# Two f32 parts in place of three bf16 parts, and two more counted groups in each layer, in a two-layer graph network on one core

## The chip, the core and the metric

The kernel runs on one of the eight cores of one Trainium2 chip. The metric is device time in microseconds (us). The core has TensorE (PE; its weight loads are listed apart as PEld), VectorE (DVE), ScalarE (ACT), GpSimd (POOL) and SyncE (SP), which issues DMAs.

## What is computed

Two mean-aggregating graph layers (SAGE), a linear layer, a residual and a layer norm. There are 12,500 nodes with 256 features and 200,000 edges, sorted by target; targets are drawn as 12500 u^2, so that low nodes have many edges.

```python
def sage(x, src, dst, W_l, b_l, W_r):
    agg = segment_sum(x[src], dst, 12500)
    deg = segment_sum(ones, dst, 12500)
    return (agg / maximum(deg, 1))[:, None] @ W_l + b_l + x @ W_r     # mean of the neighbours
h = relu(sage(x, src, dst, W1_l, b1, W1_r))
h = relu(sage(h, src, dst, W2_l, b2, W2_r))
out = layernorm(x + h @ W3 + b3)
```

## The kernel before

The edges form 1563 tiles of 128, the nodes 98 blocks of 128. In each layer the sums over neighbours come in one of two ways.

**Counted groups.** The first nodes, in groups of 256 (DN), are done by products. For a group, `count` builds a matrix of how often each of the 12,544 source rows points to each of its 256 nodes: per edge tile some VectorE comparisons (`pick`, `low`, `aft`; L738 to L746), matmuls into `count_ps` (L765 to L780) and one ScalarE copy into `counts` (L782). `product` then multiplies all 98 blocks of rows with it. The rows are f32, and the counts are whole numbers below 256. So that the sum is exact, `exact` splits each row into three bf16 parts, stored in DRAM (`x3_d`, `h3_d`); a block and a group take 3 parts x 2 halves of the features = 6 matmuls of 256 columns (L707). Layer 1 has five such groups (HG1), layer 2 eight (HG).

In layer 2 a pass does two groups at once: group 4 + i from `counts` in SBUF, and group i, whose counts layer 1 stored in DRAM (`stored`, L831) and which are streamed back into `spare` (L697). Both groups' matmuls load the same rows anew. The first pass runs alone, the two after it beside the counting of groups 6 and 7.

**Gathers.** The edges of all other nodes go in rounds of four tiles. GpSimd gathers the source rows by indirect DMA into one of four buffers `got` (L262); TensorE sums them with four strip matmuls `part_ps` (L274) and, after a ScalarE copy `some`, with the matmuls of `summed` (L290), and VectorE adds the result into a ring `sums` (L304).

**Order.** TensorE and GpSimd run in the order in which the program is written. `layer` writes it round by round: the gather's strips first, then three parts of filler, with a piece of a finished block (`pieces`: transposes, the four weight products L925 and L930, and in layer 2 those with W3, L997) at the start of each. The filler is a list of stages; `mixed` interleaves the parts of a stage in proportion to costs written by hand (COST_DENSE, COST_DEGREES, COST_SPLIT, `count_cost`), and the rounds are shared out over the stages by those costs. In layer 1, stage 0 counts group 0 beside the splitting of the rows; stage g counts group g beside the products and degrees (L797) of group g - 1 and the storing of its counts. Eight rounds in layer 1 and fourteen in layer 2 are left for after the last stage.

**The rows' ring.** SP loads the row parts of two blocks at a time into one of four buffers (NROWS), 384 KB each (L693). A load is made to wait for the gather's strip that follows the last product from its buffer:

```python
if len(used) >= n and used[-n] < len(strips):
    tc.add_manual_dep(load.ins, strips[used[-n]], LANDED, reason="products done")
```

SP also loads and stores the blocks' rows (L896, L974, L977, L1010) and the degrees (L960, L965), in one queue.

Of the kernel before, what the change touches and what calls it, by code (L numbers as in the profile page):

```python
# [1 line left out]

# [5 lines left out]
F32 = mybir.dt.float32  # L8
F16 = mybir.dt.float16
# [14 lines left out]
P = 128  # L24
# [23 lines left out]
def by_runs(  # L48
# [55 lines left out]
    HG1, HG, DN = 5, 8, 256  # L104
# [6 lines left out]
    ROOMS = [5, 5, 7, 7] + [5] * 5 + [7] * 5 + [9] * 5 + [10] * 2  # L111
# [3 lines left out]
    def room(t):  # L115
# [15 lines left out]
    x3_d = dram.tile([P, NB, 3, D], BF16, name="x3_d")  # L131
    h3_d = dram.tile([P, NB, 3, D], BF16, name="h3_d")
    count_d = dram.tile([HG1 - 1, P, NB, DN], BF16, name="count_d")
# [7 lines left out]
    place = consts.tile([1, len(groups)], I32, name="place")  # L141
# [3 lines left out]
    key_t = [consts.tile([P, n], F32, name=f"key_t{g}") for g, n in enumerate(tiles_of)]  # L145
    after_from = [max(t, FIRST - 1) for t in lows[:HG]]
    after_t = [consts.tile([P, b - a], F32, name=f"after_t{g}")
               for g, (a, b) in enumerate(zip(after_from, highs))]
    offs = [consts.tile([1, n], I32, name=f"offs{g}") for g, n in enumerate(tiles_of)]
# [33 lines left out]
    degs = spare[0:1]  # L183
    rdeg = early.tile([P, NB], F32, name="rdeg")
# [6 lines left out]
    NROWS = 4  # L191
# [380 lines left out]
    w3_sb = weight(w3, "w3_sb", "w3")  # L572

    biases = consts.tile([P, 3, D], F32, name="biases")
    for i, b in enumerate((b1, b2, b3)):
        nc.scalar.dma_start(biases[:, i], b[None, :].to_broadcast([P, D]))
# [9 lines left out]
    split = keep.tile([P, 2, 3, D], BF16, name="split")  # L586
    counts = [keep.tile([P, NB, DN + WIDEST + WIDEST % 2], BF16, name=f"counts{i}") for i in range(2)]
    NEAR = int(at_most(FIRST)) + room(FIRST - 1)
    assert NEAR <= DN
    for c_sb in counts:  # L590
        blank = c_sb.rearrange("p s d -> p (s d)").bitcast(F32)
        nc.scalar.copy(blank, zero.to_broadcast(list(blank.shape)))
# [63 lines left out]
    def exact(t, s, rest):  # L656


        def upper(a):
            return a.bitcast(BF16).rearrange("p (n h) -> p n h", h=2)[:, :, 1]  # L660

        leaves = nc.vector.tensor_tensor(rest, t, upper(t), op=OP.subtract)
        nc.vector.tensor_tensor(s[:, 2], rest, upper(rest), op=OP.subtract)
        nc.scalar.copy(s[:, 0], upper(t))
        nc.scalar.copy(s[:, 1], upper(rest))
        return leaves

    def split_rows(b):
        t = load_rows(x, N, b, "split_sb")
        s = split[:, b % 2]  # L670
        leaves = exact(t, s, work.tile([P, D], F32, name="rest", tag="own"))
        if b < 3:
            later(leaves)
        nc.sync.dma_start(x3_d[:, b], s)

    STREAMS = 4
    streams = [spare.bitcast(BF16)[:, i * 2 * DN:(i + 1) * 2 * DN].rearrange("p (b d) -> p b d", b=2)
               for i in range(STREAMS)]
    n_streamed = 0

    def product(table3, g, c_sb, beside=None):


        nonlocal n_streamed
        ps = [dense_pool.tile([P, NC, DN], F32, name="dense_ps")]
        if beside is not None:
            ps.append(beside_pool.tile([P, NC, DN], F32, name="beside_ps"))
        for t in ps:
            nc.tensor.matmul(t, lhsT=zeros_b, rhs=c_sb[:, :NC, :DN], start=True, stop=False)
        for b in range(NB):  # L690
            if b % 2 == 0:
                rows = work.tile([P, 2, 3, D], BF16, name="rows", bufs=NROWS)
                loads = [(nc.sync.dma_start(rows, table3[:, b:b + 2]), NROWS)]  # L693
                if beside is not None:
                    stream = streams[n_streamed % STREAMS]
                    n_streamed += 1
                    loads.append((nc.sync.dma_start(stream, count_d[beside, :, b:b + 2]), STREAMS))  # L697

                for load, n in loads:
                    if len(used) >= n and used[-n] < len(strips):  # L700
                        tc.add_manual_dep(load.ins, strips[used[-n]], LANDED, reason="products done")
            counted = [c_sb[:, b, :DN]] + ([stream[:, b % 2]] if beside is not None else [])
            n = 0
            for k in range(3):
                for c in range(NC):
                    for t, d in zip(ps, counted):
                        nc.tensor.matmul(t[:, c], lhsT=rows[:, b % 2, k, c * P:(c + 1) * P], rhs=d,  # L707
                                         start=False, stop=b == NB - 1 and k == 2 and c == NC - 1)
                        n += 1
                        if n == 3 * NC and beside is not None:  # L710
                            yield COST_DENSE
            if b % 2:
                used.append(len(strips))
            yield COST_DENSE
        d_sb = work.tile([P, NC, DN], F32, name="d_sb", bufs=1)
        nc.scalar.copy(d_sb, ps[0])
        yield g, d_sb
        if beside is not None:
            b_sb = split.rearrange("p two k d -> p (two k d)").bitcast(F32)[:, :NC * DN].rearrange(
                "p (c d) -> p c d", c=NC)  # L720
            nc.scalar.copy(b_sb, ps[1])
            yield beside, b_sb

    def count(g, to):
# [7 lines left out]
        def pick(t):  # L732
# [7 lines left out]
            low = work.tile([P, LW], BF16, name="low", bufs=6)  # L740
# [3 lines left out]
            if t + 1 >= FIRST:  # L744
                aft = work.tile([P, NB], BF16, name="aft", bufs=6)
# [60 lines left out]
    COST_DENSE, COST_DEGREES, COST_SPLIT = 0.7, 1.6, 0.8  # L806
# [22 lines left out]
    def stored(g, c_sb):  # L829
        for b0 in range(0, NB, 14):  # L830
            nc.sync.dma_start(count_d[g, :, b0:b0 + 14], c_sb[:, b0:b0 + 14, :DN])  # L831
            yield 0.5

    def dense(table3, waiting, with_deg, g, c_sb, beside=None):
        made = []
        for p in product(table3, g, c_sb, beside):
            if isinstance(p, float):
                yield p
            else:
                made.append(p)  # L840
        if with_deg:
            yield from degrees(g, c_sb)
        for g, d_sb in made:
# [11 lines left out]
    assert NB % 14 == 0 and HG == 2 * (HG1 - 1)  # L855

    def stages_1(waiting):

        for g in range(HG1 + 1):
# [3 lines left out]
            else:  # L863
                parts.append((dense(x3_d, waiting, True, g - 1, counts[(g - 1) % 2]), D_1))
                if g < HG1:
                    parts.append((stored(g - 1, counts[(g - 1) % 2]), MOVED))
            yield list(parts)

    def stages_2(waiting):

        for beside, g in enumerate(range(HG1 - 1, HG)):
            parts = [(dense(h3_d, waiting, False, g, counts[g % 2], beside), D_2)]
            if HG1 <= g < HG - 1:
                parts.append((count(g + 1, counts[(g + 1) % 2]), counting(g + 1)))
            yield parts
# [78 lines left out]
    def first_block(b, agg=None):  # L954
# [21 lines left out]
        exact(h, s, own)  # L976
        nc.sync.dma_start(h3_d[:, b], s)  # L977
        yield True

    def last_block(b, agg=None):  # L980
# [8 lines left out]
        h2, _ = sage(h_t, copied, b, agg, of_ring, w2l_sb, w2r_sb, biases[:, 1], "h")  # L989
# [3 lines left out]
        nc.vector.tensor_add(x_sb, x_sb, biases[:, 2])  # L993
# [405 lines left out]
```

## Time and profile before

| | |
|---|---|
| median of 3 runs | 3284.89 us (3281.76 to 3287.56) |
| profiled execution, its span | 3281.46 us, 3279.7 us |
| mean granted TensorE clock | 0.888 |
| PE busy | 2574.5 us (79%), 18946 instructions |
| POOL busy | 1967.7 us (60%) |
| DVE busy | 1566.5 us (48%) |
| ACT busy | 1151.6 us (35%) |
| DMA | 612.56 MB, mean 187 GB/s |
| of it SP's queue, the gathers' queue | 343.33 MB, 264.37 MB |
| chain that ended last | PE 59%, issue 8%, unknown queue 7%, DVE 5%, ACT 3%, DMA 3% |

Busy time is a union over an engine's instructions. Matmuls overlap: a product of 256 columns has a mean duration of 282 ns, but the next starts earlier, so the spacing of starts is what a matmul costs. A waiting time is put down to the event that ended it. A group of instructions is given as line, engine, operation, output <- inputs, shape and number.

### The profile page before, as it was taken

How to read it: one execution, taken by the hardware profiler on the slowest of the kernel's cores; microseconds unless marked ns; L12 is line 12 of the kernel's file. 1: busy time of each engine (PE TensorE's matmuls, PEld its weight loads, DVE VectorE, ACT ScalarE, POOL GpSimd, SP SyncE). 2: the span in 40 equal slices, each digit the busy share in tenths (PEclk: the TensorE clock that was granted, in tenths of full speed). 3: DMA queues.
4: the chain of work that ended last, by engine and by line, in shares of the span. 5: the costliest groups of instructions: out<-in, count | busy, mean ns of one | idle time of the engine just before them, and what ended most of it. 6: DMA issues, size and time to landing. Idle time of an engine off the chain costs nothing.

```text
span 3279.7 us, 56146 instructions
## 1 busy us (share of the span) xinstructions
PE 2574.5 (79%) x18946; PEld 1733.1 (53%) x18946; DVE 1566.5 (48%) x5560; ACT 1151.6 (35%) x2331; POOL 1967.7 (60%) x2026
## 2 busy tenths in 40 slices
PE   4565668878878878889865887878889888888876
PEld 2122335545546656656643555556556666666654
DVE  6778675544445555555552122334345444343334
ACT  0423664444444444455441001223233333221122
POOL 6665666666665656666664666565666666556652
PEclk9766679979979989989987899989989999999998
DMA  5565668658658758647644566565556656566642
GB/s 123 164 185 171 179 205 274 209 159 262 209 156 289 225 174 266 221 144 238 222 142 122 181 183 184 176 181 166 177 167 192 184 170 183 164 200 198 204 139 84
DMA packets 375242, 612.56 MB, mean 187 GB/s; under 512 B 72111, under 2 KB 253989, under 8 KB 374949
## 3 DMA queue, kind: packets, MB, share of 16 engines
q1 hardware_dynamic: 273235, 343.33, 34.0%
q0 software_dynamic: 96768, 264.37, 26.7%
q8 instruction: 155, 2.54, 0.3%
q10 hardware_dynamic: 4946, 1.19, 0.2%
q14 instruction: 138, 1.13, 0.1%
HBM read 518.75 MB, written 89.92 MB: 186 GB/s over the span
## 4 chain that ended last, share of the span: by engine, by line
PE 59%; issue 8%; another core or an unknown queue 7%; DVE 5%; ACT 3%; DMA 3%; POOL 0%; ACTq 0%; DVEq 0%; SPq 0%; POOLq 0%
PE dense_ps L707 16%; PE part_ps L274 7%; PE count_ps L776 7%; PE beside_ps L707 6%; PE block_ps L925 6%; PE block_ps L930 5%; PE sum_ps L290 4%; PE block_ps L997 3%; PE block_ps L902 3%; DMA rows<-x_d 2%; ACT counts L782 2%; PE count_ps L780 1%; PE sum_ps L296 1%; PE dense_ps L797 1%
## 5 line engine op out<-in xcount | busy, mean ns | idle before, releaser
L262 POOL DMA_INDIRECT got<-in_x_dram,src_t x1076 | 1067.8, 992 | 649.6 <-issue 258.2
L262 POOL DMA_INDIRECT got<-h_d,src_t x940 | 897.7, 955 | 617.1 <-issue 230.8
L707 PE MATMUL dense_ps<-counts,rows 128*128 128x256 bf16 x5292 | 981.6, 282 | 58.9 <-issue 31.5
L707 PEld LDWEIGHTS <-rows 128*128 128x128 bf16 x7644 | 745.2, 101 | 327.6 <-issue 165.6
L782 ACT CAST counts<-count_ps 128x882 f32 (+3 forms) x688 | 611.3, 888 | 533.1 <-PE count_ps L776 135.6
L707 PE MATMUL beside_ps<-spare,rows 128*128 128x256 bf16 x2352 | 570.3, 282 | 24.2 <-issue 23.2
L776 PE MATMUL count_ps<-pick,low 128*128 128x490 bf16 (+2 forms) x1188 | 378.7, 371 | 145.0 <-ACT counts L782 64.3
L274 PE MATMUL part_ps<-got,one 128*32 128x257 f32 (+1 forms) x4032 | 385.4, 434 | 53.2 <-issue 21.7
L738 DVE TENSOR_SCALAR pick<-steps,key_t 128x686 bf16<-128x686 f16 (+3 forms) x816 | 332.6, 410 | 117.6 <-remote 32.1
L218 DVE TENSOR_TENSOR one<-lo_t,lane_b 128x128 f32<-128x128 bf16 x504 | 144.1, 286 | 470.7 <-remote 150.1
L284 ACT COPY some<-part_ps 128x257 f32<-128x257 f32 (+1 forms) x355 | 132.8, 374 | 643.4 <-remote 293.7
L741 DVE TENSOR_SCALAR low<-lanes,low_t 128x130 bf16<-128x130 f16 x816 | 221.0, 272 | 212.4 <-remote 72.5
L304 DVE TENSOR_TENSOR sums<-sums,sum_ps 128x256 f32 x355 | 145.6, 410 | 250.2 <-remote 110.6
L290 PE MATMUL sum_ps<-two,some 128*128 128x128 f32 x1420 | 241.1, 296 | 13.1 <-issue 8.3
L290 PEld LDWEIGHTS sum_ps<-two,some 128*128 128x128 f32 x1420 | 211.2, 207 | 32.2 <-issue 19.3
L776 PEld LDWEIGHTS <-low 128*128 128x128 bf16 x1188 | 121.1, 103 | 181.9 <-issue 62.7
L936 DVE TENSOR_TENSOR own<-block_ps,biases 128x256 f32<-128x256 f32 x196 | 82.4, 420 | 220.3 <-PE block_ps L930 106.5
L274 PEld LDWEIGHTS part_ps<-got,one 128*32 128x32 f32 x4032 | 89.1, 113 | 184.1 <-issue 161.1
L925 PE MATMUL block_ps<-w1l_sb,sums 128*128 128x256 f32 x352 | 123.5, 483 | 69.7 <-issue 31.5
L933 ACT COPY sums<-zero 128x256 f32<-128x256 f32 x170 | 68.7, 404 | 306.0 <-PE block_ps L930 142.6
L904 ACT COPY own_t<-block_ps 128x256 f32<-128x256 f32 x294 | 109.3, 375 | 183.4 <-remote 65.4
L746 DVE TENSOR_SCALAR aft<-steps,after_t 128x98 bf16<-128x98 f16 x689 | 173.6, 252 | 0.0
(184 smaller groups left out, 2678.7 us busy)
## 6 DMA issues: line engine op xcount, KB each, us to landing
rows<-x_d SPq DMA_DIRECT2D x245, 384.0 KB
rows<-h_d SPq DMA_DIRECT2D x196, 384.0 KB
count_d<-counts SPq DMA_DIRECT2D x28, 896.0 KB
spare<-count_d SPq DMA_DIRECT2D x196, 128.0 KB
x_sb<-in_x_dram SPq DMA_DIRECT2D x194, 128.0 KB
x_d<-split SPq DMA_DIRECT2D x98, 192.0 KB
h_d<-split SPq DMA_DIRECT2D x98, 192.0 KB
got<-in_x_dram,src_t POOLq DMA_INDIRECT x1076
```

Of the source, the lines that this page charges most:

```text
L262: rows = nc.gpsimd.indirect_dma_start(out=g[:, j, :D], out_offset=None, in_=self.table, in_offset=bass.IndirectOffsetOnAxis(ap=src_t[:, e: ...
L274: strip = nc.tensor.matmul(part_ps[j * W:(j + 1) * W, :width], lhsT=one[:, j], rhs=g[:, j, :width], start=r == 0, stop=r == n - 1)
L290: nc.tensor.matmul(sum_ps[:, c], lhsT=some[:, c * P:(c + 1) * P], rhs=two, start=True, stop=True)
L304: nc.vector.tensor_add(own, own, sum_ps[:, :NC])
L707: nc.tensor.matmul(t[:, c], lhsT=rows[:, b % 2, k, c * P:(c + 1) * P], rhs=d, start=False, stop=b == NB - 1 and k == 2 and c == NC - 1)
L738: nc.vector.tensor_scalar(r[:, :w * NB], steps[:, :w * NB], key_t[g][:, t - lo_g:t - lo_g + 1], None, op0=OP.is_equal)
L741: nc.vector.tensor_scalar(low.rearrange("p (a b) -> p a b", a=5), lanes_5[:, :, :LW // 5], low_t[:, t:t + 1], None, op0=OP.is_equal)
L746: nc.vector.tensor_scalar(aft.rearrange("p (a b) -> p a b", a=7), steps_7[:, :, :NB // 7], after_t[g][:, t - after_from[g]:t - after_from[ ...
L776: nc.tensor.matmul(c[:, a * NB:b * NB], lhsT=s, rhs=r[:, a * NB:b * NB], start=True, stop=alone)
L782: nc.scalar.copy(to[:, :, bass.ds(off_act.at(t), w)], c.rearrange("p (d s) -> p s d", s=NB))
L925: product = nc.tensor.matmul(ps[:, 0], lhsT=agg[:, c], rhs=wl[:, c], start=c == 0, stop=c == NC - 1)
L930: product = nc.tensor.matmul(ps[:, 1], lhsT=own_t[:, c], rhs=wr[:, c], start=c == 0, stop=c == NC - 1)
```

## The change

HG1 goes from 5 to 7 and HG from 8 to 10, so that groups 5 and 6 in layer 1, and 8 and 9 in layer 2, are counted instead of gathered. A row is split into two f32 parts, the first with the low 12 bits cleared, the second the rest; the products read them as float32r, and the bf16 counts are widened to float32r by ScalarE first (`widened`). A block and a group then take 2 parts x 2 halves = 4 matmuls; in layer 2 a pass does two neighbouring groups with one matmul of 512 columns. Rows come one block (256 KB) at a time into six buffers. Layer 2 runs groups 6 and 7 from SBUF, then the stored pairs (0, 1), (2, 3), (4, 5) beside the counting of 8 and 9, then 8 and 9. COST_DENSE becomes 0.5 and COST_SPLIT 0.7. Tables share space, and W3 and b2 are loaded between the layers.

```diff
-    HG1, HG, DN = 5, 8, 256
+    HG1, HG, DN = 7, 10, 256
...
-    x3_d = dram.tile([P, NB, 3, D], BF16, name="x3_d")
-    h3_d = dram.tile([P, NB, 3, D], BF16, name="h3_d")
-    count_d = dram.tile([HG1 - 1, P, NB, DN], BF16, name="count_d")
+    x2_d = dram.tile([P, NB, 2, D], F32, name="x2_d")
+    h2_d = dram.tile([P, NB, 2, D], F32, name="h2_d")
+    SAVED = list(range(HG1 - 1)) + list(range(HG1 + 1, HG - 2))
+    count_d = dram.tile([P, NB, len(SAVED), DN], BF16, name="count_d")
...
-    NROWS = 4
+    NROWS = 6
...
-        leaves = nc.vector.tensor_tensor(rest, t, upper(t), op=OP.subtract)
-        nc.vector.tensor_tensor(s[:, 2], rest, upper(rest), op=OP.subtract)
-        nc.scalar.copy(s[:, 0], upper(t))
-        nc.scalar.copy(s[:, 1], upper(rest))
+        leaves = nc.vector.tensor_scalar(s[:, 0].bitcast(I32), t.bitcast(I32), -4096, None,
+                                         op0=OP.bitwise_and)
+        nc.vector.tensor_tensor(s[:, 1], t, s[:, 0], op=OP.subtract)
...
-    STREAMS = 4
+    STREAMS = 6
...
+    def loaded(table2, b, pair=None, ahead=0):
+        nonlocal n_streamed
+        rows = work.tile([P, 2, D], F32, name="rows", bufs=NROWS)
+        loads = [(nc.sync.dma_start(rows, table2[:, b]), NROWS)]
+        counted = both[:, b, :, :DN]
+        if pair is not None:
+            counted = streams[n_streamed % STREAMS]
+            n_streamed += 1
+            loads.append((nc.sync.dma_start(counted, count_d[:, b, pair:pair + 2]), STREAMS))
+
+        for load, n in loads:
+            n -= ahead
+            if len(used) >= n and used[-n] < len(strips):
+                tc.add_manual_dep(load.ins, strips[used[-n]], LANDED, reason="products done")
+        return rows, counted
+
+    WIDE = 3
+
+    def widened(counted):
+        wide = work.tile([P, 2, DN], F32, name="wide", bufs=WIDE)
+        nc.scalar.copy(wide.bitcast(F32R), counted)
+        return wide
+
+    def product(table2, g, c_sb):
...
+        for b in range(NB):
+            rows, _ = loaded(table2, b)
+            for u in range(b - b % 2, min(b + 2 * WIDE - 3, NB), 2):
+                if u not in wide:
+                    wide[u] = widened(c_sb[:, u:u + 2, :DN])
+            of = wide[b - b % 2]
+            for k in range(2):
                 for c in range(NC):
+                    nc.tensor.matmul(ps[:, c], lhsT=rows[:, k, c * P:(c + 1) * P].bitcast(F32R),
+                                     rhs=of[:, b % 2].bitcast(F32R), start=False,
+                                     stop=b == NB - 1 and k == 1 and c == NC - 1)
+            used.append(len(strips))
             yield COST_DENSE
...
+    def products(table2, g, pair):
...
+        for b in range(NB):
+            for u in range(b, min(b + WIDE, NB)):
+                if u not in wide:
+                    rows[u] = loaded(table2, u, pair, u - b)
+                    wide[u] = widened(rows[u][1])
+            (own, _), of = rows.pop(b), wide.pop(b)
+            for k in range(2):
+                for c in range(NC):
+                    nc.tensor.matmul(ps[c], lhsT=own[:, k, c * P:(c + 1) * P].bitcast(F32R),
+                                     rhs=of.bitcast(F32R), start=b + k == 0,
+                                     stop=b == NB - 1 and k == 1)
+                if k == 0:
+                    yield COST_DENSE
+            used.append(len(strips))
+            yield COST_DENSE
...
-    COST_DENSE, COST_DEGREES, COST_SPLIT = 0.7, 1.6, 0.8
+    COST_DENSE, COST_DEGREES, COST_SPLIT = 0.5, 1.6, 0.7
...
+        yield [passed(HG1 - 1)]
+        before = SAVED[:HG1 - 1:2]
+        for g in range(HG1 + 1, HG, 2):
+            saved = [passed(s) for s in before]
+            yield [(chain.from_iterable(p for p, _ in saved), sum(c for _, c in saved)),
+                   (next_counts((g, g + 1)),
+                    sum(counting(i) + (MOVED if i in SAVED else 0.0) for i in (g, g + 1)))]
+            before = [g]
+        yield [passed(HG - 2)]
```

## The prediction

> **What bounds the kernel now.** I read the page's groups first, then busy time by stage, then the waits, then the timeline of one gather round. The profiled execution took 3281.46 us (span 3279.7), 0.1% under the median 3284.89; all sums are made against 3281.5. A difference under 0.2% can't be told from none here.
>
> The groups (busy us, mean ns of one, idle before):
>
> ```profile
> L707 PE MATMUL dense_ps<-counts,rows 128*128 128x256 bf16 x5292 | 981.6, 282 | 58.9 <-issue 31.5
> L707 PE MATMUL beside_ps<-spare,rows 128*128 128x256 bf16 x2352 | 570.3, 282 | 24.2 <-issue 23.2
> L782 ACT CAST counts<-count_ps 128x882 f32 (+3 forms) x688 | 611.3, 888 | 533.1 <-PE count_ps L776 135.6
> ```
>
> The products (L707) are the largest work. I cut the span at the first product (478), the last product matmul of layer 1 (1638) and the first and last of layer 2 (1761, 3156):
>
> ```profile
> 0.00:478.00 478.00, 275.68 (x1291) 117.72 (x1292) 354.42 (x1263) 191.23 (x409) 301.43 (x296) 0.73 0.58 167
> 478.00:1638.00 1160.00, 972.80 (x7810) 664.28 (x7809) 605.63 (x2330) 546.30 (x1012) 717.15 (x737) 0.91 0.70 219
> 1761.00:3156.00 1395.00, 1170.09 (x8832) 844.86 (x8831) 494.67 (x1595) 335.66 (x714) 849.73 (x891) 0.93 0.60 180
> ```
>
> The columns are PE, PEld, DVE, ACT, POOL, granted clock, DMA share, GB/s. TensorE is busy 84% in both product stretches; VectorE leads only before 478. Layer 1 already uses the DMA engines 70%. TensorE's order is fixed, so work on it, and its waits, set the time. Who waits for the loads of the products' rows is in the waits of 500 to 1640 and in SP's own waits:
>
> ```profile
> PE dense_ps L707 <- DMA rows<-x_d: 26.3, 19, 5.7
> ```
> ```profile
> SPq L693 <- PE part_ps L274: 292.4, 81, 11.3
> ```
>
> So TensorE hardly waits for rows (26 us), but the loads wait for TensorE, at the gather's strips (L274). One round shows how:
>
> ```profile
> 1026.95 0.64 PE L274 MATMUL part_ps<-got,one 128*32 128x257 f32 x8
> ...
> 1030.26 0.82 SPq L693 DMA_DIRECT2D rows<-x_d  x2
> ...
> 1032.17 0.64 PE L274 MATMUL part_ps<-got,one 128*32 128x257 f32 x8
> ...
> 1035.42 0.80 SPq L693 DMA_DIRECT2D rows<-x_d  x2
> 1035.87 1.26 PE L707 MATMUL dense_ps<-counts,rows 128*128 128x256 bf16 x10 [0.80 <-DMA rows<-x_d]
> ```
>
> A strip releases the buffers of all blocks used since the strip before; SP then issues their loads in one go, here 2.7 us after the strip's end, and their first use comes 5.6 us after the issue. Over the trace, in layer 1, the issue is a median 2.0 to 3.1 us behind the strip's end (the strip's signal alone 1.05 us on average), and where TensorE waited for the load, issue to use was mostly 3.1 to 3.9 us. A load landed a median 2.0 to 3.8 us before its use: the ring of buffers is just large enough.
>
> **Part by part.**
>
> *Price of one product.* At full clock bf16 products start 0.11 us apart, and an f32 one of 256 columns is two records 0.215 us apart:
>
> ```profile
> 2954.07 0.27 PE L707 MATMUL beside_ps<-spare,rows 128*128 128x256 bf16 x1
> 2954.18 0.27 PE L707 MATMUL dense_ps<-counts,rows 128*128 128x256 bf16 x1
> 2954.29 0.27 PE L707 MATMUL beside_ps<-spare,rows 128*128 128x256 bf16 x1
> 2954.40 0.61 PE L290 MATMUL sum_ps<-two,some 128*128 128x128 f32 x4
> 2955.49 1.13 PE L997 MATMUL block_ps<-w_sb,own_t 128*128 128x256 f32 x4 [0.48 <-issue]
> ```
>
> No float32r is in this trace. Bounds for 256 columns: 0.11 (bf16) and 0.215 (one f32 record). I take 0.11: the f32 rows price operands of full width, and these parts have 12 bits. That is an assumption; the other end is a rival. Weight loads of f32 don't raise it, since the 128-column f32 records start 0.11 us apart, each with a weight load of its own. The Trainium skill (FP8 and Floating Point Precision, TensorE Precision Notes) gives f32 four passes and a reduced form that reads 4 bytes and truncates them; no run here shows that form, and at one pass it would be 0.107 us.
>
> *Dense work.* Layer 1: 5 x 588 matmuls become 7 x 392, 2940 to 2744; at the stage's average spacing of 0.122 us, 359 to 343 us. Layer 2: 4 x 1176 of 256 columns become 5 x 392 of 512; 582 to 482 us (0.124 per 256 columns).
>
> *Other TensorE work.* Groups 6 and 7 (136 tiles at 0.485 us, layer 2's rate) move to layer 1: +66. Layer 2 counts 116 tiles for 8 and 9 instead: -8. Two more degree passes: +13. Gathers fall from 1076 and 940 to 988 and 868, 22 and 18 rounds at 0.70 us with their sums (0.75 us for each of 11 and 9 groups): -24 and -19. TensorE in sum: layer 1 +39 (inside the rounds summed below), layer 2 -127.
>
> *ScalarE.* Widening adds 833 copies of 128x512 at about 0.6 us (L716: 590 ns), +500 us; splitting loses 392 copies at 0.405, -159; 116 more tiles of count copies near 1 us, +116. From 35% busy to about 45%. It is first-in first-out: behind a widening that waits for a buffer or a stream stand the count copies and the blocks' copies, for which TensorE waits. Layer 1 widens a pair ahead, layer 2 two blocks; I charge 30 us in layer 2, with 0 and 100 as ends, and nothing in layer 1, where the wait below covers it.
>
> *Set-up and first stage (to 478).* By the planner's costs this stage gets 40 of 226 rounds instead of 56 of 250. Ends: 16 rounds of VectorE work at 1.0 us (one 0.286, and in 7 of 10 rounds two of 0.336, 0.410 and 0.274), less 10 us for two more groups' tables (-6), and 16 whole rounds at 6.9 us (-110). I take -35, nearer the VectorE end since that engine is 74% busy. Splits lose two ScalarE copies each, off the bound; the AND costs VectorE at most the 0.414 us it replaces.
>
> *The rows' ring.* Here is the cost. A layer-1 stage now gets 226 x 122/1044 = 26.5 rounds (planner's costs), and products are 49 of the dense part's 71.4, so 98 blocks pass in 18.2 rounds: 5.4 blocks a round, where the trace shows 27 to 30 rounds a product, 3.3 to 3.6 blocks a round. The ring shrinks from 4 x 2 to 6 blocks. At a strip about 4.7 blocks lay ready; now 0.6. All others of the round are first asked for at its own strip. From the strip's start to the first use: 0.64 strip, 1.5 signal and SP (between 1.05 and the medians above), 3.2 load (256 KB instead of 384): 5.35 us. TensorE has some 1.7 us of work ahead of that block, so it waits about 3.65 us each round. The rest of the round's work (5.9 us: strip 0.7, sums 0.5, blocks 1.1, 2.4 count tiles 1.0, products 2.6) is 4.2 us, and loads that arrive 0.7 to 1 us apart add 0.3: 9.85 us a round, where without the ring it would be 5.9 and 1.0 of the usual waits. A product takes 18.2 x 9.85 = 179 us, less 5 for the blocks loaded ahead; the degrees' 8.3 rounds stay at 6.2, 51 us. A stage is 226 us, seven are 1582 against 1160: **+422**. With 0.6 and 3.0 us in place of 1.5, a round is 8.95 or 11.3 and the total moves by -115 or +185.
>
> SP issues single blocks: 1176 loads for 441, 0.32 us each, +235 us on a queue with time to spare; behind a waiting load stand x_sb, deg and the h stores. Layer 2 asks two blocks earlier at 2.3 to 2.7 blocks a round, so its ring holds. w3 and b2 load once between the layers behind the two weights already there: nothing. The tails (8 and 14 rounds) stay.
>
> Sum: 3281.5 - 35 + 422 + (30 - 127) = 3571.5; I say **3570**, own range 3455 to 3755.
>
> **Rivals.**
>
> *TensorE keeps the time (faster).* If early releases or SP's order give the rows in time, a round is 6.9 us, a stage 177, layer 1 +79: 3281.5 - 35 + 79 - 97 = 3229. For it: TensorE's 84%. Against it: 0.6 blocks ready at a strip. It decides below about 7.3 us a round (0.4 us of wait). Chance 0.11.
>
> *DMA bandwidth alone.* A layer-1 product moves 25.7 MB of rows, 6.4 of stored counts, 9.5 of gathers and 4.4 of blocks, 46 MB; where stages start now, the engines are full at about 325 GB/s (20 us slices), so 141 us, a stage 192, layer 1 +184: 3334. For it: 70% share now. Chance 0.13.
>
> *The ring, and a slow clock on top.* After a long wait TensorE runs at half speed:
>
> ```profile
> 1004.53 1.46 PE L707 MATMUL dense_ps<-counts,rows 128*128 128x256 bf16 x6 [5.65 <-DMA rows<-x_d]
> ...
> 1006.87 1.49 PE L707 MATMUL dense_ps<-counts,rows 128*128 128x256 bf16 x6
> ```
>
> Six products start 0.21 us apart, and still do 2.3 us on. If most waits did this, some 2 us for 127 rounds, +254: 3825. Against it: the waits would be near 3.65 us, the one seen was 5.65. The Trainium skill (TensorE: Matmul & The Clock Gate, What's actually happening) has the clock halved after an idle window of about 3.4 us; the trace agrees for 5.65 us and leaves 3.65 open. Chance 0.12.
>
> *float32r takes two passes.* 0.215 for 256 columns: +288 in layer 1, +412 in layer 2 beside the ring: 4270. The change would then not do what it says. Chance 0.07.
>
> **Numbers.** The ring as summed has 0.57. The range leaves out the faster rival and the two passes (0.18): 3300 to 3830. Slower 0.57 + 0.13 + 0.12 + 0.07 = 0.89, less 0.03 for a DMA case that ends even and 0.01 for one that wins: 0.85; same 0.03; faster 0.12.
>
> **What would show it.** Right: after 450, TensorE waits for "DMA rows" some 3 us once a round in layer 1, 300 us or more; products there last 160 us or more with 18 rounds each; layer 2's five passes end near 1300 us after the first. Wrong: products of 130 us, few waits for rows, or records 0.2 us apart for 256 columns at full clock.

## The result, and the profile after

The changed kernel takes **3712.02 us** (median of 4 runs, 3707.39 to 3716.48) where the kernel before, on the same chip, takes 3283.32 us (4 runs, 3279.32 to 3287.56). The ratio is 1.1305, with a 95% interval of 1.1285 to 1.1326: slower, as forecast, by 429 us instead of 285. The profiled execution took 3707.39 us (span 3705.6), at a granted clock of 0.85 against 0.888.

The groups, as before (busy us, mean ns of one, idle before):

```profile
L729 PE MATMUL dense_ps<-wide,rows 128*128 128x256 f32 x2744 | 578.7, 350 | 393.3 <-DMA rows<-x_d 373.2
L824 ACT CAST counts<-count_ps 128x882 f32 (+3 forms) x804 | 743.7, 926 | 482.7 <-PE count_ps L818 246.0
L712 ACT CAST wide<-counts 128x512 fp32r<-128x512 bf16 x539 | 331.3, 619 | 512.2 <-PE dense_ps L729 221.2
L752 PE MATMUL dense_ps<-wide,rows 128*128 128x512 f32 x980 | 472.6, 482 | 61.3 <-ACT wide L712 23.6
L752 PE MATMUL beside_ps<-wide,rows 128*128 128x512 f32 x980 | 407.4, 416 | 0.0
```

L729 are the products of layer 1, L752 those of layer 2, L712 the widening. The first line holds the result: ahead of layer 1's products TensorE was idle for 393 us, and 373 us of that ended with a load of rows. Before, it was 26 us. ScalarE's widening mostly waits for TensorE, not the other way round.

Busy time by stage, cut at the first product, the last of layer 1, the first and last of layer 2 (columns: PE, PEld, DVE, ACT, POOL, granted clock, DMA share, GB/s):

```profile
0.00:442.00 442.00, 239.81 (x1127) 100.56 (x1127) 336.81 (x1238) 125.62 (x180) 238.55 (x241) 0.69 0.59 175
442.00:2175.00 1733.00, 1257.84 (x8350) 892.28 (x8351) 721.23 (x2724) 835.24 (x1335) 684.65 (x710) 0.83 0.65 204
2291.00:3586.00 1295.00, 1075.46 (x5847) 735.51 (x5840) 469.74 (x1502) 581.56 (x1178) 785.27 (x820) 0.93 0.74 237
```

Layer 1's product stretch grew from 1160 to 1733 us (+573). Everything else shrank: the first stage by 36, the step between the layers by 7, layer 2's products by 100 and the tail by 4. In layer 1's stretch TensorE's idle time rose from 187 to 475 us, and its busy time from 973 to 1258. In layer 1 no engine and no queue is full: TensorE's share fell from 84% to 73%, the DMA share from 70% to 65%, and TensorE's granted clock from 0.91 to 0.83. So something is waiting in a circle. Both ends of the circle show in the waits, first of all engines in 442 to 2175, then of SP's own queue in 500 to 2175 (us in total, times, longest):

```profile
PEld dense_ps L729 <- DMA rows<-x_d: 401.9, 215, 8.5
PE dense_ps L729 <- DMA rows<-x_d: 373.2, 218, 8.3
```
```profile
SPq L695 <- PE part_ps L286: 404.8, 103, 8.4
```

TensorE waits for rows, and the loads of those rows (L695) wait for TensorE's gather strip (L286). The row of this kind that the prediction shows for the kernel before, 292.4 us, is of the whole run. From 478 to 1638 its loads (L693) waited 355 us in all, and less is put down to the strip:

```profile
SPq L693 <- PE part_ps L274: 45.8, 21, 4.7
```

The rest is put down to other TensorE work or to nothing known; there the strip as the cause rests on the code and on the round shown. The timeline of one round after, TensorE and SP alone:

```profile
997.93 0.64 PE L286 MATMUL part_ps<-got,one 128*32 128x257 f32 x8
...
998.63 2.22 SPq L695 DMA_DIRECT2D rows<-x_d  x5
...
1001.42 0.74 PE L729 MATMUL dense_ps<-wide,rows 128*128 128x256 f32 x4 [0.60 <-DMA rows<-x_d]
...
1004.23 0.74 PE L729 MATMUL dense_ps<-wide,rows 128*128 128x256 f32 x4 [1.22 <-DMA rows<-x_d]
...
1007.43 0.64 PE L286 MATMUL part_ps<-got,one 128*32 128x257 f32 x8
...
1010.86 1.22 PE L729 MATMUL dense_ps<-wide,rows 128*128 128x256 f32 x4 [1.45 <-DMA rows<-x_d]
```

The strip ends at 998.57. SP then issues five loads of 256 KB in one go. Blocks come into use one after another, two of them with a wait. The next strip can't come earlier than the products written ahead of it, so it comes 9.5 us after this one, and only then are further buffers free. The first load behind that strip is used at 1010.86, 2.8 us after the strip's end.

A second cause is mixed in. In this round a sixth load was issued only at 1003.99, although its buffer was released at 998.57 too: on SP's queue it stands behind two stores. Stores of a degree row (L1016) and of h (L1030), which wait for other engines, stand between the row loads throughout (442 to 2175):

```profile
SPq L1016 <- DVE spare L312: 237.1, 50, 11.5
SPq L1030 <- ACT h L995: 141.6, 29, 12.9
```

By the trace, 101 of the 373 us of waits were for loads that SP issued behind another transfer, although the strip had released their buffer before that. No run moves these transfers to another queue.

### The profile page after: what moved, and what is told of

The parts are those of the page before. It is cut to its first block, busy times and chain, and to the rows that moved or that the text cites. A ratio compares the mean times of both kernels' runs of the same rounds, so it can differ in the third digit from the quotient of the medians.

```text
span 3705.6 us, 53134 instructions
## 1 busy us (share of the span) xinstructions
PE 2722.9 (73%) x16330; PEld 1830.7 (49%) x16330; DVE 1637.0 (44%) x5836; ACT 1616.9 (44%) x2869; POOL 1801.5 (49%) x1866
## 4 chain that ended last, share of the span: by engine, by line
PE 51%; DMA 21%; issue 8%; DVE 8%; another core or an unknown queue 4%; ACT 4%; SPq 3%; POOL 1%; DVEq 0%; ACTq 0%; POOLq 0%
DMA rows<-x_d 16%; PE dense_ps L729 9%; PE part_ps L286 7%; PE count_ps L818 6%; PE dense_ps L752 6%; PE beside_ps L752 6%; PE sum_ps L302 4%; PE block_ps L981 4%; PE block_ps L986 3%; PE block_ps L1053 2%; SPq L695 2%; PE block_ps L958 2%; ACT counts L824 2%; DMA split_sb<-in_x_dram 2%
## 5 line engine op out<-in xcount | busy, mean ns | idle before, releaser
L274 POOL DMA_INDIRECT got<-h_d,src_t x868 | 831.1, 958 | 579.4 <-issue 215.8
L824 ACT CAST counts<-count_ps 128x882 f32 (+3 forms) x804 | 743.7, 926 | 482.7 <-PE count_ps L818 246.0
L729 PE MATMUL dense_ps<-wide,rows 128*128 128x256 f32 x2744 | 578.7, 350 | 393.3 <-DMA rows<-x_d 373.2
L729 PEld LDWEIGHTS dense_ps<-wide,rows 128*128 128x128 f32 x2744 | 453.7, 232 | 509.4 <-DMA rows<-x_d 401.9
L818 PE MATMUL count_ps<-pick,low 128*128 128x490 bf16 (+2 forms) x1420 | 492.5, 402 | 112.4 <-ACT counts L824 35.4
L712 ACT CAST wide<-counts 128x512 fp32r<-128x512 bf16 x539 | 331.3, 619 | 512.2 <-PE dense_ps L729 221.2
L752 PE MATMUL dense_ps<-wide,rows 128*128 128x512 f32 x980 | 472.6, 482 | 61.3 <-ACT wide L712 23.6
L780 DVE TENSOR_SCALAR pick<-steps,tables 128x490 bf16<-128x490 f16 (+3 forms) x932 | 384.4, 413 | 120.9 <-PE count_ps L818 47.4
L752 PE MATMUL beside_ps<-wide,rows 128*128 128x512 f32 x980 | 407.4, 416 | 0.0
L286 PE MATMUL part_ps<-got,one 128*32 128x257 f32 (+1 forms) x3712 | 340.9, 443 | 33.4 <-DMA got<-h_d,src_t 21.4
L752 PEld LDWEIGHTS dense_ps<-wide,rows 128*128 128x128 f32 x980 | 198.0, 202 | 155.3 <-issue 78.5
L230 DVE TENSOR_TENSOR one<-lo_t,lane_b 128x128 f32<-128x128 bf16 x464 | 132.9, 287 | 310.4 <-PE part_ps L286 124.1
L752 PEld LDWEIGHTS beside_ps<-wide,rows 128*128 128x128 f32 x980 | 198.7, 203 | 28.8
L788 DVE TENSOR_SCALAR aft<-steps,tables 128x98 bf16<-128x98 f16 x805 | 203.7, 253 | 0.0
```

The source lines that it names most:

```text
L274: rows = nc.gpsimd.indirect_dma_start(out=g[:, j, :D], out_offset=None, in_=self.table, in_offset=bass.IndirectOffsetOnAxis(ap=src_t[:, e: ...
L286: strip = nc.tensor.matmul(part_ps[j * W:(j + 1) * W, :width], lhsT=one[:, j], rhs=g[:, j, :width], start=r == 0, stop=r == n - 1)
L712: nc.scalar.copy(wide.bitcast(F32R), counted)
L729: nc.tensor.matmul(ps[:, c], lhsT=rows[:, k, c * P:(c + 1) * P].bitcast(F32R), rhs=of[:, b % 2].bitcast(F32R), start=False, stop=b == NB - ...
L752: nc.tensor.matmul(ps[c], lhsT=own[:, k, c * P:(c + 1) * P].bitcast(F32R), rhs=of.bitcast(F32R), start=b + k == 0, stop=b == NB - 1 and k ...
L780: nc.vector.tensor_scalar(r[:, :w * NB], steps[:, :w * NB], key_t[g][:, t - lo_g:t - lo_g + 1], None, op0=OP.is_equal)
```

## The experiments

They ran on two other chips of the same kind, on which every kernel is faster: the kernel before took 2727.72, 2744.72 and 2743.36 us beside them (one run, one run, median of 7). The first and the last are the same chip, so 0.6% is scatter there. Each is therefore read against the kernel before on its own chip, and by stage. (Expectations in absolute times were written for the chip of the result where they were not written as ratios.) Times of one run are given as such. "Product" is the time from the first to the last product matmul of a layer-1 group; in the changed kernel there are seven of them.

**The changed kernel again**, to have it on such a chip.

> The changed kernel itself, beside the kernel before on the same chip, as the measure for the runs around it. Its chip may be another than that of the first profiles. Where the four runs before this one were made, the kernel before took 2727.72 us; there I expect 3250 to 3330 us: ring5's 3477 less about 1.4 us for each of 127 rounds of layer 1's products, a product near 190 us. Ratio to before 1.19 to 1.22, where the first chip gave 1.13.

One run: 3340.34 us, ratio 1.217, just above the expected time. The seven products take 184.7 to 208.7 us, mean 198.0; on the chip of the result 189.6 to 209.2, mean 199.5. The degrees' rounds between them, in which no rows are loaded, take a mean 4.4 us instead of 6.6, and layer 2's product stretch 1100 us instead of 1294. So what sets the time of the products in layer 1 doesn't depend on what makes this chip faster, and the waits are the same:

```profile
PE dense_ps L729 <- DMA rows<-x_d: 377.1, 234, 6.4
```

**One buffer less for rows.**

```diff
-    NROWS = 6
+    NROWS = 5
```

> Five row buffers instead of six, nothing else. Theory (the ring: loads are asked for at a strip, 5.4 blocks a round against the ring's size): at a strip no block lies ready any more, a round of a layer-1 product grows from 11.1 us (199.5 us a product, mean of the seven) by 1.5 to 2 us, a product to 225 to 235 us, the time to 3890 to 3960 us. Rival (DMA bandwidth): the same bytes in the same time, 3712 us within 20. Rival (TensorE or ScalarE work): unchanged, 3712 us. Layer 2 needs 4 to 5 buffers and may lose a little in either case.

One run: 3476.98 us, some 4% more than the changed kernel on such a chip. Products 204.0 to 226.8 us, mean 215.8 (+18; the last experiment below, whose layer 1 is the changed kernel's, has a mean of 202.6, so some 5 us are scatter), and the wait for rows 443.5 us. That is less than the 25 to 35 us a product that were expected, but neither rival has any. The size of the ring counts.

**Two buffers more for rows,** with a gather buffer given up to make room.

```diff
-    NGOT = 4
+    NGOT = 3
...
-    NROWS = 6
+    NROWS = 8
```

> Eight row buffers instead of six; their room in SBUF comes from the gathers, which get three buffers instead of four. Ring: 2.6 blocks ready at a strip instead of 0.6, a round of a layer-1 product near 9 us, a product 160 to 170 us, in all about 3450 to 3520 us, less what the gathers lose by the missing buffer (GpSimd already waits for TensorE most of the time, so little in layer 1; in layer 2 up to 50 us). DMA bandwidth: no gain, 3712 us or above. TensorE or ScalarE work: no gain, 3712 us or above.

One run: 3057.27 us. Products 143.7 to 163.1 us, mean 154.8, a little under the expected 160 to 170; the wait for rows 193.5 us. Two more buffers shorten a product by 43 us, although each gather now has a buffer less.

**Loads released by the last product of their own buffer,** not by the strip behind it. Layer 2's row loads are freed as well; its streams keep the strip.

```diff
-            if len(used) >= n and used[-n] < len(strips):
+            if n == STREAMS - ahead and load is not loads[0][0] and len(used) >= n and used[-n] < len(strips):
```

> The added dependency of a row load on the gather's strip is left out; the load still waits for the products that read its buffer. Ring: buffers come free half a round earlier on average and one by one, a round near 8.5 to 9.5 us, a product 155 to 175 us, 3430 to 3560 us. If the products' own end can only be signalled late (TensorE's signals were seen 1 us late on average), less. DMA bandwidth: 3712 us. If the strip is not what the loads wait for: 3712 us.

One run: 2905.32 us, ratio 1.065. Products 124.1 to 144.0 us, mean 138.0, where 155 to 175 were expected. The waits change hands (all engines, then SP's queue):

```profile
PE dense_ps L729 <- DMA rows<-x_d: 110.3, 73, 4.7
```
```profile
SPq L695 <- PE dense_ps L729: 170.9, 191, 3.0
...
SPq L695 <- PE part_ps L286: 18.0, 38, 1.8
```

SP now waits for single products, and the strip is nearly gone from its waits (747 us in the changed kernel on such a chip). Buffers and bytes are those of the changed kernel. So of the loss on these chips, the release rule is about 0.152 of the time before (1.217 less 1.065, each on its own chip), some 415 us; layer 1's stretch alone falls from 1612 to 1191 us. What then holds the products shows in the windows of this kernel (columns as above):

```profile
1000.00:1020.00 20.00, 17.54 (x130) 13.16 (x130) 10.27 (x36) 13.19 (x20) 10.83 (x12) 0.98 0.99 334
1020.00:1040.00 20.00, 18.31 (x135) 13.70 (x136) 10.81 (x43) 14.78 (x26) 12.38 (x13) 1.00 1.01 332
...
1100.00:1120.00 20.00, 19.39 (x233) 13.35 (x230) 17.32 (x70) 16.58 (x29) 15.25 (x15) 1.00 0.67 209
```

Beside products the DMA engines are full, at 332 to 334 GB/s; beside degrees (the last line) they are not. Over whole products the share is 0.95 to 0.99, at 315 to 331 GB/s. The prediction's 46 MB a product over 332 GB/s is 139 us, and 138 was measured. One rival is left: 104 of the 110 us that TensorE still waits are for loads that SP issued behind another transfer, and no run tells a late issue from a full DMA.

**Half the bytes of the rows.** Layer 1 loads the first part alone, and it stands for both in the products, so the sums there are those of the first part twice.

```diff
-        loads = [(nc.sync.dma_start(rows, table2[:, b]), NROWS)]
+        loads = [(nc.sync.dma_start(rows[:, 0], table2[:, b, 0]) if pair is None and table2 is x2_d else nc.sync.dma_start(rows, table2[:, b]), NROWS)]
...
-                    nc.tensor.matmul(ps[:, c], lhsT=rows[:, k, c * P:(c + 1) * P].bitcast(F32R),
+                    nc.tensor.matmul(ps[:, c], lhsT=rows[:, 0, c * P:(c + 1) * P].bitcast(F32R),
```

> In layer 1 only the first part of the rows is loaded, 128 KB instead of 256 a block, and it stands for both parts in the products (the second part is left out of the result); ring, waits and matmuls as they were. Ring: only the landing gets shorter, a product 180 to 190 us, 3590 to 3650 us. DMA bandwidth: 12.9 of 46 MB a product are gone, a product 145 to 155 us, 3320 to 3400 us.

One run: 3041.63 us. Products 146.4 to 159.8 us, mean 155.1; the wait for rows 204.3 us. This is a miss for the ring theory as it stood: it had 180 to 190 us, and the rival of DMA bandwidth had 145 to 155. The bytes count for 43 us a product, though the DMA engines are not full: over these products their share is 0.70 to 0.72 in the first six and 0.62 in the last. What fits is that the loads of a round are issued together, so that a later one lands after all before it have been moved. Where TensorE waited, the first load behind a strip was used a median 2.2 us after the strip's end instead of 2.8 (the changed kernel on such a chip), the third 4.3 instead of 6.5. With half the bytes a product still takes 17 us more than with all bytes and single releases.

**ScalarE's widening.** Layer 1 widens one pair of counts for each group and uses it for all 98 blocks, so the other counts are left out.

```diff
-                    wide[u] = widened(c_sb[:, u:u + 2, :DN])
+                    wide[u] = widened(c_sb[:, u:u + 2, :DN]) if u == 0 else wide[0]
```

> In layer 1 only the first pair of blocks of a product is widened and stands for all the others (the rest of the counts is left out of the layer's sums): 336 of 343 copies of ScalarE are gone, the loads, waits and matmuls are as they were. Ring: no change, within 40 us of the changed kernel, products the same length, TensorE's wait for rows the same or longer. Rival (ScalarE: the widening holds up the count copies and the blocks): at least 150 us less.

One run: 3355.85 us, 0.5% above the changed kernel on that chip; the wait for rows is 385.9 us. 336 copies fewer (ACT busy 1434 us for 1617) bring nothing: the widening is hidden in layer 1.

**The format alone:** two float32r parts with their ring of six single blocks and their planner's costs, but five and eight groups.

```diff
-    HG1, HG, DN = 7, 10, 256
+    HG1, HG, DN = 5, 8, 256
```

> The changed kernel with five and eight counted groups as before: the format alone. A product of layer 1 then has about 27 rounds, 3.6 blocks a round, so 2.4 of 6 blocks lie ready at a strip. Ring: waits of 0.5 to 1 us a round at most, layer 1's five products near 27 x 6 to 6.5 us, and with four passes of 512 columns the whole within 3% of the kernel before on the same chip, either side: most of the loss comes from the two added groups. Rival (the format itself, float32r with widening and 33% more bytes a row, costs it): at least 8% slower than before.

One run: 2850.24 us, ratio 1.038, just outside what was expected. Products take 170.9 to 179.0 us. Their 24 to 27 rounds use up the ring more slowly than 17 to 19 rounds do, and the wait is 164.9 us for five products (33 each) instead of 377.1 for seven (54 each). So of the 596 us lost on that chip, the format with its ring costs 106 and the two more groups in each layer 490. Most of the latter goes through the same ring, since with single releases the groups cost 0.064 (1.065 above less 1.001 below, some 175 us): more groups mean fewer rounds of gathers, hence fewer strips to release buffers, and more blocks to release at each.

**The same with single releases** (both edits above).

> c58 without the row loads' dependency on the gather's strip. Ring: the rest of the waits goes, 50 to 150 us less than c58, and 2 to 6% less than the kernel before on the same chip. If c58 has no such waits: the same as c58.

One run: 2747.71 us, ratio 1.001. The release is worth 102 us here, as expected (50 to 150), but no gain on the kernel before is left, where 2 to 6% were expected. Products take 146.0 to 163.1 us, as in the kernel before with the same edit (145.5 to 167.6, below), though a group has 392 matmuls for 588. Two things fit. A float32r matmul costs more than was forecast (see below): from a matmul's start to the next one's, idle time left out, the five products take TensorE 302 us, and 334 in the kernel before with that edit. And a product's rows grow from 19.3 to 25.7 MB, so the share of the DMA engines is 0.95 to 1.00 over the five products (0.84 to 0.95 in the kernel before with that edit). The second and third product (columns as above):

```profile
644.00:790.00 146.00, 130.44 (x964) 96.44 (x965) 81.23 (x314) 94.03 (x165) 110.66 (x117) 0.94 1.00 342
845.00:997.00 152.00, 128.81 (x937) 96.97 (x936) 80.36 (x303) 92.24 (x162) 102.86 (x108) 0.92 0.98 325
```

**The kernel before with single releases.**

```diff
-                    if len(used) >= n and used[-n] < len(strips):
+                    if load is not loads[0][0] and len(used) >= n and used[-n] < len(strips):
```

> The kernel before without its row loads' dependency on the strip. Its ring holds 8 blocks against 3.4 a round, so by the ring theory there is little to gain: within 1.5% of before. If the strip held the kernel before as it holds the changed one: over 3% faster.

One run: 2725.2 us, 0.7% less than the kernel before (2743.36, median of 7), and hardly more than the scatter on that chip. With its eight blocks in the ring and 3.3 to 3.6 used in a round, the strip hardly holds it.

**Degrees as a lighter load.** In the two kernels with single releases the products have the DMA engines nearly full, while the degrees have DMA to spare. COST_DEGREES lowered to 0.5 moves gather rounds from the degrees to the products.

```diff
-    COST_DENSE, COST_DEGREES, COST_SPLIT = 0.5, 1.6, 0.7
+    COST_DENSE, COST_DEGREES, COST_SPLIT = 0.5, 0.5, 0.7
```

With seven and ten groups:

> nostrip (seven and ten groups) with the same planner's price of 0.5. A stage of layer 1 moves 52 MB, 158 us at 331 GB/s, where nostrip took 139 + 38: 50 to 130 us less than nostrip, ratio to before 1.02 to 1.05 (nostrip: 1.065). Rival (TensorE's work): as nostrip.

One run: 2867.71 us, ratio 1.045 (1.065 without this edit). That is 38 us less, where 50 to 130 were expected. The products take 137.1 to 156.9 us, the degrees 16.8 to 22.0. With five and eight groups:

> c58_nostrip with the planner's price of a degree step at 0.5 instead of 1.6, so that the products spread over 87% of a stage instead of 69%. Theory (without the strip, a layer-1 product is held by DMA bandwidth: 46 MB in 139 us were 331 GB/s, while the degrees' part of a stage moves little): a stage of layer 1 falls from 207 us to 185 to 195, 60 to 110 us less than c58_nostrip; ratio to the kernel before 0.96 to 0.98. Rival (TensorE's work holds the products): as c58_nostrip, ratio 1.00.

Four runs: 2699.5 us (2698.56 to 2701.3), ratio 0.9837 with a 95% interval of 0.9807 to 0.9866. That is 48 us less than without the edit (one run, on the other chip), where 60 to 110 were expected. It is 1.6% less than the kernel before: a small gain, clear of the scatter of four and seven runs, and 0.9% less than the one run of the kernel before with single releases.

**Layer 2 without the second part's products,** so that TensorE has half the product work there. The last block keeps them.

```diff
-                for c in range(NC):
+                for c in range(NC if k == 0 or b == NB - 1 else 0):
```

> The changed kernel with the second row part's matmuls left out of layer 2's products (980 of 1960, that part is left out of the result); loads, widening and gathers as they were. If TensorE holds layer 2, its five passes get shorter until the DMA engines are full: 340 MB at 331 GB/s are 1030 us, so 40 to 100 us less on a chip where they took 1100 us, and up to 250 us less where DMA leaves room. If the gathers' pace holds it (a round takes what four gathers take): unchanged within 15 us, 217 rounds at the same time each.

One run: 3316.63 us, 24 us less than the changed kernel on the other chip. By stage, layer 1 is 30 us longer there and layer 2's product stretch falls from 1100 to 1047 us. These 53 us lie in the range expected if TensorE holds layer 2 (40 to 100) and outside that of the gathers' pace (15). But TensorE's time in layer 2's products, waits left out, fell by 219 us (546 to 327), of which only 53 were gained, and the DMA engines, which were to be the next limit, are at a share of 0.89. The first three passes take 5.0 to 5.1 us a round (5.1 to 5.4 without the edit), the last two fall from 5.8 and 5.7 to 5.4 and 5.2. The first of the waits of 2139 to 3239, in the changed kernel on such a chip, suggests who sets that pace:

```profile
POOL got L274 <- issue: 207.4, 679, 0.6
```

GpSimd, which gathers, has 0.3 us between gathers in which it waits for nothing that the profile shows; with its 783 us of busy time it is occupied for 990 of 1100 us, or some 5 us for a round of four gathers. So on these chips both hold layer 2: TensorE above all in the last two passes, and below it, at some 5 us a round, the gathers' pace. No run makes the gathers faster, so the second half is argued.

## Why the prediction was right, and where it was off

**Set-up and first stage: -35 forecast, -36 measured.** The first product starts at 442.5 us for 478.4. The match is partly luck: I had picked the figure between -6 and -110 by VectorE's work, and VectorE's busy time there fell by 18 us. TensorE's idle time is 202 us in both kernels (478 less 275.7, 442 less 239.8), and its own work fell by 36.

**The price of float32r: 0.11 us for 256 columns forecast; 0.118 inside a run of products, but 0.154 on average at full clock.** Where TensorE is not slowed, four product matmuls last 0.74 us and eight 1.21 to 1.28, so one more costs about 0.12. One of 512 columns costs 0.23 us, as here in the timeline of layer 2:

```profile
3002.25 0.39 PE L752 MATMUL beside_ps<-wide,rows 128*128 128x512 f32 x1
3002.48 0.40 PE L752 MATMUL dense_ps<-wide,rows 128*128 128x512 f32 x1
3002.72 0.39 PE L752 MATMUL beside_ps<-wide,rows 128*128 128x512 f32 x1
```

That is within a tenth of bf16's rate, so the rival of two passes (0.215 for every one) is out. But the step from a block's first product to its second is longer: a median 0.222 us at full clock, 0.118 for the next two (454, 462 and 467 of them). The bf16 products of before have no such step (eight in ten are 0.108 to 0.111 us apart). Counted from a matmul's start to the next one's, idle time left out, a layer-1 product took 0.154 us at full clock and 0.185 over all, where the sum had 0.122. The weight loads may be the reason (a mean 232 ns each, 101 for bf16), against what the prediction argued; that was not tried.

**ScalarE: nothing in layer 1, 30 us in layer 2.** The first is borne out by the run without widening. In layer 2 TensorE was idle 24 us that ended with a widening (23.6 in the first line of L752 above); how much of that reached the end was not tried.

**The rows' ring: +422 forecast, +573 measured. This is the term that was mis-sized.** Of the 422, 39 were to be TensorE's own work and 383 waits. Measured are 285 (busy 972.8 to 1257.8 us) and 288 (idle 187 to 475). The products took TensorE 507 us for 359 (343 forecast), counting 284 for 177 (+107 for +66). The mechanism is shown: the wait and its place in the traces, +18 us a product with a buffer less, -43 with two more, -60 with single releases. The rounds were forecast well, 18.2 a product where 17 to 19 were written. A round was forecast at 9.85 us and took 11.2 on average (1396 us of products over 125 rounds), and 125 times 1.3 us are 165 us; six phases of degrees lie in the stretch, of 52 to 59 us, where the sum had seven of 51. Inside the round two terms were off, in opposite directions:

- The wait was over-sized. From strip to first use I had 5.35 us with 1.5 us for the signal and SP and 3.2 for the load; in the round shown it is 3.4 us (strip 0.64, then 2.8), over 119 rounds a median 3.5. SP issued the first load a median 0.06 us after the strip's end, not 1.5. The waits for rows sum to 3.0 us a round (373.2 over 125) instead of 3.65, and they are not one wait but 1.7 a round.
- The rest of the round was under-sized: 6.2 us forecast, 8.2 measured. I let loads arrive 0.7 to 1 us apart; behind a strip, with five loads and the gathers at once, the first came into use a median 2.8 us after the strip's end, the third, where TensorE waited for it, 6.5 us and the fourth 7.7, so 1.2 to 1.9 us apart; and half the bytes take back 43 us a product. And I priced a layer-1 product matmul at 0.122 us, the stage's average of before. They took 0.185 (0.154 at full clock, 0.252 at half): for 21.6 in a round, some 1.4 us.

**The slow clock, a rival at 0.12, is part of that second term.** The result, 3712, lies 142 us above the sum's 3570 and 113 below this rival's 3825. It was set against because the waits would be near 3.65 us, and the one that slowed the clock was 5.65. The trace shows that shorter ones do it as well:

```profile
1507.31 0.74 PE L729 MATMUL dense_ps<-wide,rows 128*128 128x256 f32 x4 [1.32 <-DMA rows<-x_d]
1508.60 0.81 PE L729 MATMUL dense_ps<-wide,rows 128*128 128x256 f32 x4 [0.55 <-DMA rows<-x_d]
...
1510.18 1.08 PE L286 MATMUL part_ps<-got,one 128*32 128x257 f32 x8
```
```profile
1506.00:1509.00 3.00, 1.14 (x7) 0.94 (x8) 1.18 (x6) 0.82 (x2) 0.00 (x0) 1.00 0.80 296
1509.00:1512.00 3.00, 3.00 (x16) 1.38 (x16) 1.11 (x4) 1.98 (x3) 0.44 (x1) 0.52 0.02 5
```

Waits of 1.32 and 0.55 us with four matmuls between them leave TensorE busy for 1.14 of 3 us, and the next 3 us run at a granted 0.52: the strip takes 1.08 us instead of 0.64. (The DMA engines are at 0.02 there: every free buffer is loaded, and nothing moves until that strip.) The Trainium skill (TensorE: Matmul & The Clock Gate, What's actually happening) has an activity monitor over windows of some 3.4 us; read as a window of low activity and not as one unbroken idle time, this trace agrees with it, and the prediction's reading was too narrow. Over layer 1's stretch the clock, whose records come in steps of 3.41 us, fell to half 104 times and stood there for 597 of 1733 us. In the step ahead of such a fall TensorE was busy for a median 41% (at most 63%), and its longest idle time in it was a median 2.0 us; in the steps at whose end the clock stayed full it was busy for a median 79% (at least 43%). In the kernel before it fell 36 times in layer 1 (200 of 1160 us), with a longest idle time of a median 2.1 us, so that trace could have shown that no wait of 5.65 us is needed.

How much of the +573 the clock costs stays open: no run changes the clock alone, and where the next load is late anyway a slower product costs nothing. The changed kernel on such a chip and the one with single releases give an estimate. Their layer-1 stretches hold the same matmuls (columns as above):

```profile
433.00:2045.00 1612.00, 1207.90 (x8352) 868.39 (x8353) 716.74 (x2723) 832.24 (x1336) 685.15 (x709) 0.85 0.69 220
429.00:1620.00 1191.00, 1045.08 (x8351) 777.52 (x8351) 701.09 (x2721) 810.84 (x1335) 685.65 (x709) 0.94 0.90 297
```

Of the 421 us between them 258 are TensorE's idle time, and 163 are the same matmuls taking less time, with the clock at half for 145 us instead of 482.

**DMA bandwidth alone, at 0.13,** was a floor and not the bound. It gave 141 us a product, and 138 is what a product takes once the strip no longer releases the loads. The changed kernel can't reach this floor in bursts. **TensorE keeps the time** (products in rounds of 6.9 us) is seen nowhere in it.

**Layer 2: -97 forecast, -100 measured, but the reason doesn't hold.** I had TensorE's work fall by 127 us, 100 of it by fewer and wider products, and 30 lost again. The products did not get cheaper: counted from start to start, idle time left out, 581.6 us before and 581.1 after, where 482 were forecast. TensorE's busy time still fell by 95 us (1170.1 to 1075.5), elsewhere: the blocks' own matmuls from 298 to 245 us for the same number of matmuls, which the sum didn't have and for which no run shows the reason, the gathers from 222 to 192, counting from 66 to 57. So the size came out by chance. In rounds, the stretch has 201 for 220, at 6.44 us each against 6.34.

What holds layer 2 on the slower chip was not tried. GpSimd's own pace doesn't: it has the same 5 us of work and issue for a round of 6.4, and it waits for TensorE in the product stretch (2291 to 3586):

```profile
POOL got L274 <- PE part_ps L286: 162.2, 67, 7.1
```

## What to carry to other kernels

When buffers are released at a slower event than their own last use (here once a round), what counts is buffers against uses per release: eight blocks and 3.5 a round cost no more than the scatter, six and 5.4 a round cost some 15% of the kernel's time, and a change that thins out the releasing event (fewer gathers) spends the same ring faster. A late release also makes bursts, so bytes begin to count while the DMA engines are a third idle on average. So before an engine's work is cut, ask in each stage which event frees the buffers and how many uses lie between two of them. And price a new operand format as the kernel issues it, four products at a time between other work, and not by the spacing inside a long run: here the difference took up all that the fewer products were to save.

## What the runs showed of the hardware

Two things I had not expected. Chips differ: the kernel before takes 3283 us on one and 2728 to 2752 on two others. On the first a strip's signal is recorded a mean 1.1 us after the strip's end in layer 1 of the kernel before, on the others 0.04 us (layer 1 of the changed kernel). The chip is not all of it: in layer 1 of the changed kernel on the first chip it is a mean 0.36 us and a median 0.04. Rounds without loads take 6.6 and 4.4 us. Gains in one stage therefore differ from chip to chip, while the ring's products are equally long. And TensorE's clock can halve after 3 us in which it was busy 38% of the time, though the longest wait ahead of a matmul in them was 1.32 us; over layer 1 it fell mostly where TensorE had been busy for less than half of a 3.41 us step.
